# Mixing 32x64 and 32x32 matmul products within a round of a four-layer convolution stack

## The chip, the cores and the metric

The kernel runs on one NeuronCore of a Trainium2 chip. The metric is the device time of one execution in microseconds; lower is better. Before the change it is 5016.14 us, the median of 3 runs (5004.99 to 5017.03).

## The reference

The input is 4 images of 16 channels, 512 x 512, in fp32. Four layers follow one another, each `x = x + f(groupnorm(x))` with 8 groups. Layers 0 and 1 are those that the change touches:

```python
def _denoise_block(x, w1, b1, w2, b2, w3, b3, a, b, c):
    trip = _triplets(x)                # each frame with the one before and the one after it
    xf = trip.reshape(B * T, C, H, W)  # 3 input channels, 1 output channel
    o = a * _conv_reflect(xf, w1, b1, 1, 2) + b * _conv_reflect(xf, w2, b2, 2, 4) + c * _conv_reflect(xf, w3, b3, 4, 8)
    return jnp.tanh(o).reshape(B, T, H, W)
# layer 0: two such blocks, 5x5 taps at dilations 1, 2 and 4
y = _denoise_block(gn(x), ...); z = _denoise_block(y, ...)
# layer 1: activations rounded to 8-bit steps, a 3x3 convolution 16 -> 16 channels, scale and bias
x_q = jnp.round(jnp.clip(x_cl / scale_input, -n, n))
acc = lax.conv_general_dilated(x_q, w_hwio, window_strides=(1, 1), padding=((1, 1), (1, 1)), ...)
out = acc * (scale_input * scale_weight) + bias
```

Layer 2 is a 17 x 17 box filter, layer 3 a complex convolution between an FFT and its inverse.

## The kernel before

**Tiling of the array.** TensorE's 128 x 128 array is used in tiles. In layers 0 and 1 each product contracts over one strip of 32 rows (`i` = 0 to 3 in layer 0, `b` = 0 to 3 in layer 1) and writes either 64 output columns (a 32x64 product, "wide", W below) or 32 (a 32x32 product, "narrow", N below). A column half `j` (columns 0 to 63 or 64 to 127) holds one W or two N. A *round* fills the whole array once: with 8 W, or with 16 N. All moving operands are 512 fp32 columns.

**Layer 0** (`Layer0`) runs 32 groups (2 convolution blocks, 4 images, 4 groups of 4 frames), each in 6 *slots*, one for each of 6 transformed frames (`ORDER`); so 192 slots. `slot` writes down by hand, in one order for all engines, what a slot does: `products` puts the slot's products on TensorE, into one of two PSUM tiles `m`; `gather` and `activated` combine the results of the slot before on ScalarE and VectorE; `late`, `early` and `fetch` prepare later frames; `transfers` issues the slot's DMAs on SyncE, each behind one of the slot's *marks* (the last product of each round), so that they spread over the slot.

The products of a slot are listed by two constants at the top of the file. `PAIRS` has 5 pairs of neighbouring shifts that one W does together, `ALONE` 4 single shifts in 2 twos, of which each half does two N. With `e` = 0 and 1 that makes 10 rounds of W and 4 of N: 10 x 8 + 4 x 16 = 144 products. `order` runs all rounds of one shape and then all of the other, W first in slots of even `p`, N first in odd ones, so that neighbouring slots meet in the same shape. `start` is set in round 0, `stop` in the last.

**Layer 1** (`layer1`, inner function `products`) runs 64 chunks `u` of 8 image rows. A chunk has 8 rounds: for each of 4 weight blocks `d` (three taps and the residual) one round of W (`both`) and one of N (`single`). Again all four rounds of one shape come first, W first in odd chunks, N first in even ones. Loads and stores are tied to marks in the same way. `rounded` and `write` run beside it on ScalarE and VectorE.

## Time and profile before

| What | us |
|---|---|
| median of 3 runs | 5016.14 |
| the profiled execution, own time | 5011.86 |
| its span, first to last instruction | 5010.0 |
| layer 0's products (L579), first start to last end | 62.2 to 2785.9 |
| layer 1's products (L1047), first start to last end | 2825.8 to 3347.9 |
| layers 2 and 3 | about 3348 to 5010 |
| mean granted TensorE clock | 0.977 of full speed |

In the profile PE stands for the matmuls, PEld for the weight loads that go with them, DVE for VectorE, ACT for ScalarE, POOL for GpSimd and SP for SyncE; `L579` is a line of the kernel. A group's name such as `32*64 32x512 f32` gives the tile of the array (rows x columns) and the moving operand. The ends of matmuls are modelled, their starts are recorded. `l0w` are layer 0's weights, `frame` its inputs, `l1q` and `l1x` layer 1's inputs.

### The profile page before, as it was taken

Reading aid. Unit: us, or ns where it says so; the run is one execution under the profiler, and the core shown is the slowest. Engines: PE = TensorE matmul, PEld = TensorE weight load, DVE = VectorE, ACT = ScalarE, POOL = GpSimd, SP = SyncE. Lnnn points to the kernel's source line nnn. Section 1 sums busy time; section 2 is a strip of 40 time slices with the busy share of each in tenths; the row PEclk is TensorE's granted clock in tenths of the full one; section 3 lists DMA queues with packets and bytes.
Section 4 is the critical chain, followed back from the end, with each engine's and each line's share of the span. In section 5 each row is a group of like instructions: output and inputs, shape, how many; then the busy total and the mean of one; then the engine's idle time right before and its main releaser. Section 6 shows DMA issues by size and latency. Waiting matters only on the chain.

```text
span 5010.0 us, 201323 instructions
## 1 busy us (share of the span) xinstructions
PE 4727.3 (94%) x90224; PEld 2673.6 (53%) x90224; DVE 4068.3 (81%) x4639; ACT 2565.3 (51%) x4220; POOL 21.5 (0%) x90
## 2 busy tenths in 40 slices
PE   4899999999999999999999699989999989999999
PEld 1344444444444444434434345548878767777776
DVE  8888888979769999999899666655555588888887
ACT  3465656563324443444434555545444456666665
POOL 0000000000000000000000000000000000000000
PEclk9999999999999999999999899999999989999999
DMA  5656565563567777776875688876666655555553
GB/s 175 166 159 167 170 164 160 152 179 96 122 139 158 152 159 160 158 160 140 168 153 135 169 276 264 263 227 230 214 217 203 207 135 146 149 144 142 151 147 115
DMA packets 393825, 850.69 MB, mean 170 GB/s; under 512 B 70912, under 2 KB 86400, under 8 KB 384512
## 3 DMA queue, kind: packets, MB, share of 16 engines
q1 hardware_dynamic: 385456, 827.22, 61.9%
q8 instruction: 707, 11.58, 1.1%
q10 hardware_dynamic: 7504, 10.60, 0.8%
q14 instruction: 158, 1.29, 0.1%
HBM read 497.51 MB, written 340.03 MB: 167 GB/s over the span
## 4 chain that ended last, share of the span: by engine, by line
PE 76%; DVE 15%; DMA 4%; issue 2%; ACT 2%; SPq 1%; ACTq 0%; POOL 0%; DVEq 0%
PE m L579 38%; PE l1p L1047 10%; PE l2p L1154 8%; PE u L1622 5%; PE s L1563 5%; PE u L1563 4%; DVE frame L487 4%; PE u L1585 2%; PE pt L1597 2%; DVE frame L432 2%; DVE l2o L1194 2%; PE l2p L1205 1%; DVE st L1195 1%; DMA frame<-y 1%; DVE B L630 1%
## 5 line engine op out<-in xcount | busy, mean ns | idle before, releaser
L579 PE MATMUL m<-frame,l0w 32*64 32x512 f32 (+1 forms) x55296 | 2614.3, 612 | 171.6 <-DVE frame L527 62.2
L579 PEld LDWEIGHTS m<-frame,l0w 32*64 32x64 f32 (+1 forms) x55296 | 1180.2, 119 | 1604.8 <-issue 1379.8
L487 DVE SCALAR_TENSOR_TENSOR frame<-frame,frame 128x2376 f32<-128x2376 f32 x232 | 607.7, 2628 | 8.6
L1047 PE MATMUL l1p<-l1q,l_wt 32*32 32x512 f32 (+1 forms) x9216 | 432.9, 603 | 45.5 <-DVE l1q L1034 39.9
L1194 DVE TENSOR_TENSOR l2o<-l2x,l2p 128x512 f32<-128x512 f32 x256 | 172.6, 674 | 265.2 <-PE l2p L1154 265.2
L712 ACT ACTIVATE junk<-xb,neg 128x1024 f32<-128x1024 f32 x256 | 293.6, 1147 | 81.5 <-DVE top L691 31.7
L1047 PEld LDWEIGHTS l1p<-l1q,l_wt 32*32 32x32 f32 (+1 forms) x9216 | 188.5, 113 | 250.5 <-issue 210.8
L1154 PEld LDWEIGHTS l2p<-k_c_band,l2y 128*128 128x128 f32 x2048 | 256.7, 190 | 75.8 <-issue 55.1
L1183 ACT COPY l2y<-l2p 128x512 f32<-128x512 f32 x256 | 149.9, 586 | 282.0 <-PE l2p L1154 281.9
L1154 PE MATMUL l2p<-k_c_band,l2y 128*128 128x144 f32 (+1 forms) x2048 | 284.1, 292 | 6.0
L432 DVE STREAM_TRANSPOSE frame<-xp 128x1056 f32<-128x1056 f32 x128 | 261.5, 2126 | 29.9 <-ACT xp L401 29.9
L1154 PE MATMUL l2p<-k_c_band,l2n 128*128 128x144 f32 (+1 forms) x2048 | 267.8, 291 | 14.1 <-DMA l2x<-x 7.1
L1154 PEld LDWEIGHTS l2p<-k_c_band,l2n 128*128 128x128 f32 x2048 | 261.1, 196 | 15.0 <-ACT l2n L1172 11.1
L1622 PE MATMUL u<-k_c_hil,zt 128*128 128x128 f32 x2048 | 255.9, 278 | 0.0
L1622 PEld LDWEIGHTS u<-k_c_hil,zt 128*128 128x128 f32 x2048 | 238.4, 192 | 2.1 <-issue 0.8
L1598 ACT COPY zt<-pt 128x512 f32<-128x512 f32 x256 | 131.4, 599 | 208.3 <-PE pt L1597 208.3
L1528 DVE TENSOR_TENSOR xc<-l3n,k_c_tab 128x2048 f32<-128x2048 f32 x64 | 146.7, 2292 | 107.3 <-ACT l3n L1512 107.3
L1062 ACT ACTIVATE l1o<-l1p,k_l_bias,l_osc 128x1024 f32<-128x1024 f32 x128 | 147.2, 1200 | 137.9 <-PE l1p L1047 132.3
L1641 DVE SCALAR_TENSOR_TENSOR l3o<-u,l3t 128x256 f32<-128x256 f32 x512 | 192.3, 425 | 22.3 <-ACT l3t L1633 19.5
L1064 DVE BATCH_NORM_STATS2 l1st<-l1o 128x6 f32<-128x512 f32 x256 | 158.1, 680 | 54.1 <-ACT l1o L1062 54.1
L1028 ACT ACTIVATE l1t<-l1x,l1own,l1own 128x1024 f32<-128x1024 f32 x128 | 151.7, 1233 | 89.9 <-DMA l1x<-x 83.6
L1047 PE MATMUL l1p<-l1x,l_wt 32*32 32x512 f32 (+1 forms) x3064 | 195.4, 594 | 0.0
(314 smaller groups left out, 6341.6 us busy)
## 6 DMA issues: line engine op xcount, KB each, us to landing
y<-y SPq DMA_DIRECT2D x256, 264.0 KB
xb<-in_x SPq DMA_DIRECT2D x512, 128.0 KB
x<-l1o SPq DMA_DIRECT2D x256, 256.0 KB
l2x<-x SPq DMA_DIRECT2D x64, 1024.0 KB
x<-l2o SPq DMA_DIRECT2D x64, 1024.0 KB
l3x<-x SPq DMA_DIRECT2D x256, 256.0 KB
out<-l3o SPq DMA_DIRECT2D x256, 256.0 KB
l1x<-x SPq DMA_DIRECT2D x252, 256.0 KB
```

What stands on the lines that cost most here:

```text
L432: nc.vector.transpose(v[:, :, :, h, 1:17].rearrange("p k u m -> p k m u"), xp)
L487: self.nc.vector.scalar_tensor_tensor(o, x, f, y, ALU.mult, ALU.add)
L579: return nc.tensor.matmul(ps[at, i, :].rearrange("p (k c m) -> p k c m", k=nc_, c=2), w[PX * i : PX * i + PX, weights], source(i, d, e, j) ...
L712: nc.scalar.activation(junk, xs[h], f, bias=neg, accum_out=self.out_sums[b][n][:, 2 * t + h : 2 * t + h + 1])
L1028: nc.scalar.activation(t[:, at], x[:, at], AF.Identity, bias=own[1], scale=own[0])
L1047: ins = nc.tensor.matmul(ps[at : at + hi - lo, b, :], wt[rows, d, lo:hi], qs[v % 3][rows, k, d : d + W] if d < 3 else raws[v][rows, k], st ...
L1064: nc.vector.bn_stats(st[b][:, u, :], o[:, b, :])
L1154: nc.tensor.matmul(ps[:, lo:hi], lhs[:, k, at : at + P], band[:, j : j + hi - lo], start=(k == 0), stop=(k == 3), skip_group_check=True,)
L1194: nc.vector.tensor_add(o[:, hb, :], xt[:, hb, :], ps)
L1563: nc.tensor.matmul(ps[b][32 * j : 32 * j + 32], f[rows, n, j, :], x[rows, j, :], start=(i == 0), stop=(i == 2 and tag == "s"), skip_group_ ...
L1622: nc.tensor.matmul(po[:, bass.ts(k, P)], zt[:, b, k ^ 1, :], hil[:, k, :], start=False, stop=(k == 3), skip_group_check=True,)
L1641: nc.vector.scalar_tensor_tensor(o[:, v].rearrange("p k u -> p u k"), po[:, HW:W].rearrange("p (u k) -> p u k", u=2), s, t.rearrange("p (u ...
```

## The change

Each column half now has its own list of rounds. `SINGLES` says in which of a slot's 14 rounds half 0 and half 1 do their N; the two sets have no round in common. So a slot has 8 mixed rounds, in which one half does W and the other N (4 W and 8 N), and 6 rounds of W alone. Within a round the code still goes through the row strips `i` and, in each, through the halves `j`; a mixed round therefore runs W, N, N, W, N, N, ... or N, N, W, N, N, W, ... along the strips. The order no longer depends on the slot's parity. In layer 1 every round is mixed: in even rounds half 0 does N and half 1 W, in odd ones the other way round. The products, their weights, operands and results are the same in number and kind, as are the marks.

```diff
--- before.py
+++ after.py
@@ -32,6 +32,7 @@
 PAIRS = ((4, 0), (2, 1), (0, 2), (-2, 3), (1, 5))
 ALONE = (((-4, 4), (6, 0)), ((-1, 6), (3, 5)))
 NPB = 2 * len(DELTA)
+SINGLES = (0, 4, 7, 11), (2, 5, 9, 12)
 NQ = 6
 ORDER = (1, 2, 3, 4, 0, 5)
 KN = 9 * 264
@@ -561,8 +562,11 @@
         ps = self.psum.tile([P, 4, 512], F32, name=f"m{self.now}", tag="m")
         v = gr["v"][q]
         w = self.w[q]
-        runs = [(e, pair) for e in range(2) for pair in PAIRS], [(e, two) for e in range(2) for two in ALONE]
-        order = [(wide, *what) for wide in ((1, 0) if p % 2 == 0 else (0, 1)) for what in runs[1 - wide]]
+        order = []
+        for singles in SINGLES:
+            pairs = [(e, *pair) for e in range(2) for pair in PAIRS]
+            alone = [(e, two) for e in range(2) for two in ALONE]
+            order.append([alone.pop(0) if n in singles else pairs.pop(0) for n in range(14)])
 
         def source(i, d, k, j):
             if conv:
@@ -581,20 +585,21 @@
                 w[PX * i : PX * i + PX, weights],
                 source(i, d, e, j),
                 start=(n == 0),
-                stop=(n == len(order) - 1),
+                stop=(n == 13),
                 skip_group_check=True,
             )
 
-        for n, (wide, e, what) in enumerate(order):
-            base = len(DELTA) * PX * e
+        for n in range(14):
             for i in range(4):
                 for j in range(2):
-                    if wide:
+                    e, *what = order[j][n]
+                    base = len(DELTA) * PX * e
+                    if len(what) == 2:
                         d, o = what
                         at = base + PX * o
                         ins = product(slice(64 * j, 64 * j + 64), i, slice(at, at + 64), d, e, j, n)
                         continue
-                    for u, (d, o) in enumerate(what):
+                    for u, (d, o) in enumerate(what[0]):
                         at = base + PX * o
                         out = slice(64 * j + PX * u, 64 * j + PX * u + PX)
                         ins = product(out, i, slice(at, at + PX), d, e, j, n)
@@ -1036,10 +1041,10 @@
             def products(u):
                 ps = psum.tile([P, B, W], F32, name=f"l1p_{u}", tag="ps")
                 marks.clear()
-                both = ((0, 0, 0, 64), (64, 2, 0, 64))
-                single = ((0, -1, 32, 64), (32, 1, 0, 32), (64, 1, 32, 64), (96, 3, 0, 32))
-                order = [(tiles, d) for tiles in ((both, single) if u % 2 else (single, both)) for d in range(4)]
-                for n, (tiles, d) in enumerate(order):
+                wide = ((0, 0, 0, 64),), ((64, 2, 0, 64),)
+                single = ((0, -1, 32, 64), (32, 1, 0, 32)), ((64, 1, 32, 64), (96, 3, 0, 32))
+                for n in range(8):
+                    d, tiles = n // 2, (*(single, wide)[n % 2][0], *(wide, single)[n % 2][1])
                     for b in range(B):
                         for at, k, lo, hi in tiles:
                             v, k = (u - 1, 3) if k < 0 else (u, k)
```

## The prediction

> **What bounds the kernel now.** I read the busy shares first, then the chain of work that ended last, then the matmul groups with shapes kept apart.

> ```profile
> PE 4727.3 (94%) x90224; PEld 2673.6 (53%) x90224; DVE 4068.3 (81%) x4639; ACT 2565.3 (51%) x4220; POOL 21.5 (0%) x90
> PE m L579 38%; PE l1p L1047 10%; PE l2p L1154 8%; PE u L1622 5%; PE s L1563 5%; PE u L1563 4%; DVE frame L487 4%; PE u L1585 2%; PE pt L1597 2%; DVE frame L432 2%; DVE l2o L1194 2%; PE l2p L1205 1%; DVE st L1195 1%; DMA frame<-y 1%; DVE B L630 1%
> L579 PE MATMUL m<-frame,l0w 32*64 32x512 f32 x30720 | 1720.8, 598 | 70.3 <-DVE frame L527 62.2 <-DVE frame L487 4.2 <-issue 3.9
> L579 PE MATMUL m<-frame,l0w 32*32 32x512 f32 x24576 | 907.0, 629 | 101.4 <-DVE frame L487 52.8 <-issue 39.0 <-DVE C L637 8.7
> ```

> TensorE is nearly always busy, and 48% of the chain is the two lines that the change reorders (L579, L1047). The counts give the passes: 192 slots x 144 products = 27,648, yet 55,296 matmuls ran, so a product is two passes, each with its own weight load. What sits close behind TensorE in layer 0 is VectorE, 642 us of the last 685:

> ```profile
> 2100.00:2785.00 685.00, 657.03 (x13815) 295.15 (x13807) 642.45 (x615) 299.25 (x518) 0.00 (x0) 0.98 0.70 149
> ```

> The question is what a change of product shape costs, so I read layer 1's timeline, where tile names keep neighbouring rows apart (columns: start, length, then the instructions):

> ```profile
> 2999.43 1.06 PE L1047 MATMUL l1p<-l1x,l_wt 32*32 32x512 f32 x12
> 3000.42 2.83 PE L1047 MATMUL l1p<-l1q,l_wt 32*64 32x512 f32 x48
> 3003.05 1.06 PE L1047 MATMUL l1p<-l1x,l_wt 32*64 32x512 f32 x16
> 3003.91 2.78 PE L1047 MATMUL l1p<-l1q,l_wt 32*64 32x512 f32 x48
> 3006.48 1.06 PE L1047 MATMUL l1p<-l1x,l_wt 32*64 32x512 f32 x16
> 3007.48 2.98 PE L1047 MATMUL l1p<-l1q,l_wt 32*32 32x512 f32 x82
> ```

> Where the shape stays, the next row starts 0.20 us before the modelled end of the last (3003.05 against 3000.42 + 2.83); at both changes of shape only 0.06 to 0.07 before it. In the single records that distance is 0.070 us (to 0.002) at practically all of the 192 changes in layer 0 and 64 in layer 1, measured from the product that started last, wherever in the array it sat, although the starts of the last burst spread over 0 to 0.39 us. At the end of a 32x32 run the last product is in row strip 3 of column half 1; the next 32x64 one is in strip 0 of half 0, shares no cell with it, and still waits. Its weights wait too. The stretch ahead of the change at 1493.66, and one of the same length inside the new run (columns: length, then busy time and count of PE and of PEld on L579):

> ```profile
> 1493.14:1493.65 0.51, 0.51 (x18) 0.00 (x0) 1.00 0.69 225
> 1494.16:1494.67 0.51, 0.51 (x24) 0.26 (x16) 1.00 0.83 265
> ```

> No load at all for half a microsecond, against 16. I read it as one mode for the whole array: a change of shape waits until every product in flight has ended.

> **The change, part by part.** It adds and removes no product, load, transfer or wait: still 80 products of 32x64 and 64 of 32x32 in each slot, 14 marks for the transfers to hang on (8 in a layer-1 chunk), and the same VectorE, ScalarE, GpSimd and SyncE queues. What changes is how often the shape alternates in TensorE's stream. Before, 193 stretches of one shape in layer 0 and 65 in layer 1. In the built program of the changed kernel there are 12,288 in layer 0: 6,144 of two 32x32 products, 4,608 of one 32x64, 768 of eight, 384 of two and 384 of ten; and 3,585 in layer 1: 1,538 of two 32x32, 255 of four, 1,536 of one 32x64, 256 of two. A mixed round is W N N W N N ... along the four row strips (W wide, N narrow), so it has about eight changes.

> A stretch costs its first pass to its second on the same tile, then from the last start to the first start of the next shape. Both are in the records: after the change at 1493.661 the second 32x64 pass starts at 1494.141 (0.480, the weights not preloaded); after the one at 1511.471 the second 32x32 pass at 1511.926 (0.455). The second pass has its weights and lasts 0.587; less 0.070 makes 0.517, which is layer 1's start-to-start at a change. Neighbours start 0.007 apart. So one W: 0.480 + 0.517 = 0.997 us; two N: 0.455 + 0.007 + 0.517 = 0.979; two W 1.004; eight W 1.043; four N 0.993; ten W, where two tiles come twice, two more passes of 0.434, so 1.872.
> Layer 0: 6,144 x 0.979 + 4,608 x 0.997 + 768 x 1.043 + 384 x 1.004 + 384 x 1.872 = 12,515 us. Layer 1: 1,538 x 0.979 + 255 x 0.993 + 1,536 x 0.997 + 256 x 1.004 = 3,547.
> Against that, their products now take 62.2 to 2785.9 = 2,723.7 us and 2825.8 to 3347.9 = 522.1. The rest of the 5,010.0 us span is 1,764.2 and isn't touched. Sum: 1,764 + 12,515 + 3,547 = 17,826, with the 1.9 us around the span (5,011.86 profiled) 17,828: I say 17,830. The median of the runs shown is 0.1% above the profiled run, far below any bound here.

> What the change could win is inside this sum. A pure 32x32 round took 8.184 us for eight (1.02 each) against 0.88 for a 32x64 round (17.28 for 19.5), since sixteen small products with their loads come one per 17 ns twice over. That, 4 x 0.14 us a slot, is 110 us in layer 0, and is lost entirely if the array drains within each round. The other engines hide nothing of it: VectorE's 12 to 13 us a slot lie under a slot of 12,515 / 192 = 65 us. Transfers hang on marks that come later, and so does the SyncE queue behind them, but their readers are later by as much.

> [...]

> **The rivals.** (a) Free: a change waits only for the tiles it overlaps, and the halves go their own ways. Decided by whether the first W starts while the other half's N are in flight. For it: equal-shaped tiles do overlap. Against it: the 0.070 us above. Price: a slot of 14 x 0.884 = 12.4 instead of 13.27 us (17.81 + 8.72 for two slots undisturbed), at most -170 us in layer 0, of which VectorE (2,430 of its 2,724 us busy) may leave half; layer 1 about 64 x (4 x 0.14 + 0.3) = -55. So 4,790 to 4,880, say 4,830: faster.
> (b) Each half remembers its shape, so only a half's own change drains. Then a slot has about 12 single and 2 double drains. A drain between whole rounds costs 17.81 - 40 x 0.442 = 0.13 to 8.72 - 8.18 = 0.53 us, a double one 1.0 more: 12.4 + 6.6 = 19.0 us a slot, +930; layer 1, double at all eight rounds, +610. About 6,550. Nothing in the trace separates halves; it is against the loads' standing still for everything.
> (c) Full drain, and the clock stays at half. The clock was low only behind idle stretches of 2.5 us and more, and the drains leave 0.1. But a busy TensorE was seen with a low clock:

> ```profile
> 4035.00:4040.00 5.00, 5.00 (x16) 3.45 (x16) 4.20 (x6) 0.59 (x1) 0.00 (x0) 0.50 0.28 48
> ```

> and no row shows a stream with only one or two tiles of the array at work. A pass takes 1.053 there instead of 0.587: 16,062 x 1.79 + 1,764 = 30,500.

> **How the numbers follow.** Full drain at full clock 82%, (c) 4%, (b) 6%, (a) 7%, nothing measurable 1%. The likeliest case alone: at least 0.441 + 0.517 = 0.958 a stretch with the loads hidden, 17,300 us; at most 0.480 + 0.552, the longest common start-to-start, and 0.1 for what no row shows, 20,000. Stretched to 16,000 and 21,000 for passes that pair otherwise than I think and for some time at a low clock, it holds eight in ten alone; no bound of another case lies near. Faster by over 0.3% is (a): 7%; within 0.3%, about what this measurement can tell from no change: 1%; slower 92%.

> **What would show it.** Right: slots of 65 us; the idle of PEld counted under "issue" up many times over; PEld and PE with the same counts; VectorE's share near 25%, its busy time unchanged; clock near 1. One row strip's W and N starting within 0.02 us of each other would make it wrong at once: then (a). Slots near 19 us are (b), matmuls of 1.05 us (c).

## The result

The changed kernel takes 32,147.5 us (median of 4 runs, 32,146.46 to 32,151.41) against 5,016.59 before (median of 4), a ratio of 6.4099 with a 95% interval of 6.4008 to 6.419. The forecast was 17,830, in a range of 16,000 to 21,000: slower, as forecast, but 1.8 times the forecast and far outside the range.

From the page of the changed kernel: the busy shares, the clock in 40 slices (9 is nine tenths or more), and the chain of work that ended last, by engine and by line:

```profile
PE 31982.9 (99%) x90224; PEld 5169.4 (16%) x90224; DVE 4079.0 (13%) x4639; ACT 2555.7 (8%) x4220; POOL 21.3 (0%) x90
...
PEclk9999999999999999999999999999999999999999
...
PE 99%; DVE 1%; issue 0%; DMA 0%; SPq 0%; ACT 0%; ACTq 0%; DVEq 0%
PE m L583 74%; PE l1p L1052 21%; PE l2p L1159 1%; PE u L1627 1%; PE s L1568 1%; PE u L1568 1%; PE u L1590 0%; PE pt L1602 0%; DVE l2o L1199 0%; PE l2p L1210 0%; DVE st L1200 0%; PE pr L1612 0%; SPq L211 0%; DMA x<-xb 0%; DMA l0w<-frame 0%
```

The counts of instructions are those of before, and so is the work of VectorE and ScalarE. TensorE alone sets the time, with 74% of the chain in layer 0's products and 21% in layer 1's. Now the two groups of layer 0 with shapes kept apart (after the count: busy us, mean ns of one):

```profile
L583 PE MATMUL m<-frame,l0w 32*64 32x512 f32 x30720 | 12759.9, 1082 | 0.0
L583 PE MATMUL m<-frame,l0w 32*32 32x512 f32 x24576 | 11777.0, 1056 | 62.5 <-DVE frame L528 62.5
```

Before, the same matmuls had 598 and 629 ns. Nearly all now have 1,055 to 1,110, the length that some 1,300 of them had before, nearly all while the clock stood at 0.5. Yet the PEclk row shows full speed, and the mean granted clock is given as 0.999. That row can't be believed here: the trace's list of clock entries holds none before 30.5 ms, where layer 2 begins, and a time without an entry counts as full speed. The kernel before shows the same on a small scale: its list begins at 66.9 us, and the 40 matmuls that ended before that took 1,056 ns and more, though the row counts them at full speed.

The pause at a change of shape is there as foreseen, and scaled. Two stretches of the same length on L583 of the changed kernel, ahead of a change and from it on (length, busy time and count of PE and of PEld, then PEclk, DMA share and GB/s):

```profile
9001.28:9002.25 0.97, 0.97 (x16) 0.00 (x0) 1.00 0.37 135
9002.26:9003.23 0.97, 0.97 (x12) 0.18 (x4) 1.00 0.00 0
```

No weight is loaded for 0.97 us, until the last product has ended, then two narrow ones start with their loads. The stretches of one shape are just those counted from the program: 12,288 and 3,585. Two N take 1.847 us from their first start to the next shape's (6,144 times, 11,346 us), one W 1.893 (4,608 times, 8,724 us), and the next start comes 0.070 us before the modelled end of the last product, as before. Layer 0's stretches come to 23,673 us and layer 1's to 6,710, counted to the start of the last one in each; with the untouched 1,764 that is 32,148 of a span of 32,149.6. So nothing else was added, and the question left is why every pass ran at half speed.

### The profile page after: what moved, and what is told of

It is laid out like the page before. It is cut to its first block, busy times and chain, and to the rows that moved or that the text cites. A ratio compares the mean times of both kernels' runs of the same rounds, so it can differ in the third digit from the quotient of the medians.

```text
span 32149.6 us, 201322 instructions
## 1 busy us (share of the span) xinstructions
PE 31982.9 (99%) x90224; PEld 5169.4 (16%) x90224; DVE 4079.0 (13%) x4639; ACT 2555.7 (8%) x4220; POOL 21.3 (0%) x90
## 4 chain that ended last, share of the span: by engine, by line
PE 99%; DVE 1%; issue 0%; DMA 0%; SPq 0%; ACT 0%; ACTq 0%; DVEq 0%
PE m L583 74%; PE l1p L1052 21%; PE l2p L1159 1%; PE u L1627 1%; PE s L1568 1%; PE u L1568 1%; PE u L1590 0%; PE pt L1602 0%; DVE l2o L1199 0%; PE l2p L1210 0%; DVE st L1200 0%; PE pr L1612 0%; SPq L211 0%; DMA x<-xb 0%; DMA l0w<-frame 0%
## 5 line engine op out<-in xcount | busy, mean ns | idle before, releaser
L583 PE MATMUL m<-frame,l0w 32*32 32x512 f32 (+1 forms) x55296 | 23674.9, 1070 | 62.5 <-DVE frame L528 62.5
L583 PEld LDWEIGHTS m<-frame,l0w 32*32 32x32 f32 (+1 forms) x55296 | 3094.8, 171 | 20641.0 <-issue 20575.2
L1052 PE MATMUL l1p<-l1q,l_wt 32*32 32x512 f32 (+1 forms) x9216 | 5154.1, 1065 | 38.3 <-DVE l1q L1039 36.9
L1052 PE MATMUL l1p<-l1x,l_wt 32*32 32x512 f32 x3064 | 1798.6, 1065 | 0.0
L1052 PEld LDWEIGHTS l1p<-l1q,l_wt 32*32 32x32 f32 (+1 forms) x9216 | 640.6, 157 | 4442.5 <-issue 4439.3
L635 DVE TENSOR_TENSOR B<-A,m 128x1024 f32<-128x1024 f32 x64 | 77.9, 1218 | 3670.4 <-PE m L583 3670.4
L641 DVE TENSOR_TENSOR D<-C,m 128x1024 f32<-128x1024 f32 x64 | 78.0, 1218 | 3543.2 <-PE m L583 3543.2
L1035 DVE TENSOR_SCALAR l1q<-l1t 128x2048 f32<-128x2048 f32 x64 | 78.5, 1227 | 3512.4 <-PE l1p L1052 3512.3
L1052 PEld LDWEIGHTS l1p<-l1x,l_wt 32*32 32x32 f32 x3064 | 220.7, 157 | 1462.1 <-issue 1462.1
L691 DVE STREAM_TRANSPOSE zr<-z 128x1024 f32<-128x1024 f32 x128 | 151.5, 1222 | 1296.7 <-ACT z L666 1296.7
L1159 PE MATMUL l2p<-k_c_band,l2n 128*128 128x144 f32 (+1 forms) x2048 | 269.5, 292 | 14.2 <-DMA l2x<-x 7.2
```

The costliest lines, as they stand in the source:

```text
L583: return nc.tensor.matmul(ps[at, i, :].rearrange("p (k c m) -> p k c m", k=nc_, c=2), w[PX * i : PX * i + PX, weights], source(i, d, e, j) ...
L691: nc.vector.transpose(zr[:, h].rearrange("p s (k j) -> p k s j", j=16), z.rearrange("p (k r) -> p k r", r=32))
L1052: ins = nc.tensor.matmul(ps[at : at + hi - lo, b, :], wt[rows, d, lo:hi], qs[v % 3][rows, k, d : d + W] if d < 3 else raws[v][rows, k], st ...
L1159: nc.tensor.matmul(ps[:, lo:hi], lhs[:, k, at : at + P], band[:, j : j + hi - lo], start=(k == 0), stop=(k == 3), skip_group_check=True,)
```

## The experiments

All but the last two kernels leave layer 0 as before, so that layer 1 alone is asked; it lies behind 40 us in which TensorE is idle and begins with the clock at 0.5 (2790.7 to 2835.1 in the trace before). Before, its products took 522 us. Each of these kernels was run once; the last two have 4 and 10 runs. `...` marks lines left out of an edit.

**Layer 1 mixed alone.** The changed kernel's loop for layer 1 in the kernel before:

```diff
...
+for n in range(8):
+    d, tiles = n // 2, (*(single, wide)[n % 2][0], *(wide, single)[n % 2][1])
     for b in range(B):
         for at, k, lo, hi in tiles:
```

> Layer 0 as before, layer 1 mixed as in the changed kernel. In the changed kernel layer 1's 3,585 stretches of one shape took 6,711 us, all at the slow pass of 0.85 us. Theory 'asleep by its own pattern' (a layer that mixes within a round cannot keep or get the full clock): layer 1 again 6,710 us, total 5,012 - 522 + 6,710 = 11,200. Rival 'inherited' (the clock was lost in layer 0, and layer 1 only kept what it found): stretches of 0.98 to 1.00 us, layer 1 about 3,550, total 8,040.

Measured: 11,215.1 us, layer 1 6,712. The slow clock comes with layer 1's own order, whatever layer 0 did. Here the list of clock entries is complete, and it says so. A stretch of 100 us within layer 1 (columns: length, then busy time and count of PE, PEld, DVE, ACT and POOL, the clock, DMA share, GB/s):

```profile
3000.00:3100.00 100.00, 100.00 (x186) 12.37 (x184) 4.93 (x6) 4.56 (x4) 0.00 (x0) 0.50 0.05 13
```

TensorE is busy for all of it at a clock of 0.50, with only 186 matmuls.

**Half the layer pure, half mixed.**

```diff
 order = [(tiles, d) for tiles in ((both, single) if u % 2 else (single, both)) for d in range(4)]
+if u >= NYB // 2:
+    mixed = (*single[:2], both[1]), (both[0], *single[2:])
+    order = [(mixed[n % 2], n // 2) for n in range(8)]
```

> Layer 0 as before; layer 1's chunks 0 to 31 as before, chunks 32 to 63 mixed, so that the mixing begins with the clock at full. 'Wake only' (a mixed stream cannot raise the clock, but an awake array stays awake, since the drains leave it idle for only 0.1 us): 32 chunks of 55.4 us instead of 8.15, total about 6,530. 'Asleep by its own pattern': the clock falls within some 10 us of the first mixed chunk, 32 chunks of 105 us, total about 8,110.

Measured: 8,111.7 us. The clock falls, 3.4 us after the first mixed product, at 3102.8 (same columns):

```profile
3096.00:3099.00 3.00, 3.00 (x115) 1.84 (x97) 0.06 (x1) 2.38 (x2) 0.00 (x0) 1.00 0.96 285
3099.30:3102.40 3.10, 3.10 (x33) 0.51 (x8) 2.99 (x4) 2.30 (x2) 0.00 (x0) 1.00 0.79 254
3103.10:3107.00 3.90, 3.90 (x9) 0.60 (x10) 2.00 (x3) 2.37 (x2) 0.00 (x0) 0.50 0.00 1
```

The first line is the last pure chunk, the second the first mixed stretches at full clock, the third the same order at half. In the second, the two stretches that lie wholly in the full clock, one of each kind, took 0.979 us (two N) and 0.997 (one W), to the nanosecond what the forecast had. The next takes 1.144, as the clock falls in it, and from 3103.1 on they take 1.85 and 1.89, for good.

**The same rounds, half by half.** All N of one half, then all W of the other (`single` and `wide` as in the change):

```diff
...
-for b in range(B):
-    for at, k, lo, hi in tiles:
+halves = ((single[0], wide[1]), (single[1], wide[0]))[n % 2]
+for b, tiles in [(b, tiles) for tiles in halves for b in range(B)]:
+    for at, k, lo, hi in tiles:
```

> Layer 0 as before; layer 1 mixed, but in each round all N of the one column half (8 products) run before all W of the other (4 products): 16 stretches a chunk instead of 56, each filling half of the array, with the same pause at each change. Full drain at each change holds in any case. 'Fill' (the clock goes by how much of the array is at work): somewhere between; at full clock a stretch is about 1.02 us, layer 1 about 1,045 and the total 5,540. 'Pauses' (it goes by the share of time in which products stream, 0.85 of 1.0 us as in the mixed rounds): half clock, 1.92 us a stretch, layer 1 1,965, total 6,460.

Measured: 5,540.45 us, layer 1 1,048, at full clock. Each stretch has the pause of the mixed ones and is as long (1.018 us); it only has all four row strips of a half at work instead of one:

```profile
3000.00:3100.00 100.00, 100.00 (x1184) 18.94 (x1190) 42.30 (x103) 29.64 (x27) 0.00 (x0) 1.00 0.41 130
```

Pauses are out as the cause of the slow clock. That N and W stand in different halves, with no cell in common, spares no pause: of 1,023 changes here, 1,020 have 0.516 to 0.520 us from the last start to the next, and the first three, still at half clock, 0.985 to 0.987.

**Whole rounds in turn.** N and W rounds alternate, eight changes a chunk:

```diff
-order = [(tiles, d) for tiles in ((both, single) if u % 2 else (single, both)) for d in range(4)]
+order = [(tiles, d) for d in range(4) for tiles in (single, both)]
```

> Layer 0 as before; layer 1 with rounds of one shape throughout, but N and W rounds in turn: 8 changes of shape a chunk instead of 1, each stretch a whole round that fills the array, of the same length in time (two passes and a drain) as a mixed stretch. 'Fill': full clock, 4 x (1.04 + about 1.2) = 9 us a chunk, layer 1 575, total about 5,070. 'Pauses': half clock as in the mixed rounds, 15.8 us a chunk, layer 1 1,010, total 5,500.

Measured: 5,059.02 us, layer 1 563, at full clock. An N round with its change takes 1.093 us, a W round 1.078, so that seven further changes a chunk cost 0.6 us. A change between rounds that fill the array is cheap, 0.09 us each here. An estimate from layer 1 of the trace before comes near: 0.517 us from the last start to the first of the next shape, less the 0.434 from one W pass to the next on its tile, is 0.083.

**No pauses, less of the array.** One change of shape a chunk as before, but row strip after row strip, then tile after tile (in these two and the next two kernels the marks are set at eight even distances in a chunk's products):

```diff
-for n, (tiles, d) in enumerate(order):
-    for b in range(B):
+# l1_strip
+order = [(4 * s + d, b, d, shapes[s]) for s in range(2) for b in range(B) for d in range(4)]
+# l1_tile
+order = [(4 * s + d, b, d, (t,)) for s in range(2) for b in range(B) for t in shapes[s] for d in range(4)]
+for n, b, d, tiles in order:
```

> Layer 0 as before; layer 1 with the shapes in the order of before (one change a chunk), but one row strip after the other, so that a quarter of the array is at work and nothing pauses. If TensorE doesn't look past a strip: 64 passes of 0.442 us a chunk at full clock, layer 1 1,810 us, total 6,300; at half clock 3,630 and 8,120. 'Fill' with a threshold under a quarter, or 'pauses and fill together': full clock. 'Fill' with a threshold above a quarter: half clock.

> The same, but tile after tile: the products of one tile follow one another, an eighth (W) or a sixteenth (N) of the array at work, as in a mixed stretch, but without pauses and with one change of shape a chunk. If TensorE doesn't look past a tile: 192 passes of 0.442 us a chunk, layer 1 5,430 us, total 9,920 at full clock; 10,900 and 15,400 at half. 'Fill alone': half clock. 'Pauses and fill together': full clock.

Measured: 6,535.24 and 10,004.82 us; layer 1 2,032 and 5,511, both at half clock throughout. The strip order:

```profile
3000.00:3100.00 100.00, 100.00 (x628) 30.05 (x624) 16.51 (x21) 16.63 (x15) 0.00 (x0) 0.50 0.26 83
```

TensorE is never idle, changes shape once in some 32 us, and still gets half the clock. No pauses are needed for that. Both times fell between the two that were expected, because later products did start ahead of earlier ones (look-ahead): tile after tile, two matmuls ran at a time, 0.007 us apart; strip after strip, 64 W passes in 15.7 us and 128 N passes in 16.0 make 3.5 W tiles of 8 and 6.8 N tiles of 16 at work, 43% of the array both times. Within a strip only 2 W or 4 N tiles have products, so those of the next strip start while earlier ones still wait. It showed among products of one shape only: all 64 changes of the strip order have 0.985 to 0.987 us from the last start to the next, the full pause at half clock.

**Column after column.** The same, with all four row strips next to one another in the order:

```diff
-order = [(4 * s + d, b, d, shapes[s]) for s in range(2) for b in range(B) for d in range(4)]
+order = [(4 * s + d, b, d, (t,)) for s in range(2) for t in shapes[s] for d in range(4) for b in range(B)]
```

> Layer 0 as before; layer 1 without pauses as in the strip order, but one column tile after the other, all four row strips in each. The strip order had 43% of the array's tiles at work (64 W and 128 N passes of 0.853 us in 31.75 us a chunk), yet stayed at half clock, while by-halves with 45% at that clock woke. 'Share of tiles': the same 43%, half clock, layer 1 about 2,030 us, total 6,530. 'Share of row strips' (all four at work here and in by-halves, one to two of four in the strip order): full clock, layer 1 about 1,030, total 5,530.

Measured: 5,321.23 us, layer 1 828, at full clock:

```profile
3000.00:3100.00 100.00, 100.00 (x1492) 42.44 (x1488) 42.41 (x52) 34.84 (x31) 0.00 (x0) 1.00 0.51 165
```

Faster than either figure, since look-ahead filled more of the array for W than expected (64 passes of 0.427 us in 4.6 us, 74% of the tiles). But the clock rose at 2831.1, 4 us after the first product, with N alone and little more than a quarter of the tiles at work. All entries in the list of clocks lie on a grid of 3.41 us (in the kernel before the low ones last 3.41, 6.83, 10.24 us and so on); the table has, from the single records, the last steps before the clock rose, and steps of orders in which it didn't; each matmul counts as 0.853 us, the distance between two on the same tile at half clock:

| order, step of 3.41 us at half clock | share of the tiles at work | share of the time with any pass | matmuls started | then |
|---|---|---|---|---|
| columns, 2827.7 | 0.28 | 1.0 | 20 | rose |
| by halves, 2834.7 | 0.44 | 0.91 | 24 | rose |
| by halves, 2831.3 | 0.28 | 0.65 | 18 | stayed low |
| strips, W, steady | 0.49 | 1.0 | 14 to 16 | stayed low |
| strips, N, steady | 0.48 | 1.0 | 28 to 32 | stayed low |
| tiles, N, steady | 0.12 | 1.0 | 7 or 8 | stayed low |
| mixed, steady | 0.11 to 0.18 | 0.91 to 0.95 | 4 to 10 | stayed low |

Neither the share of the tiles (0.28 rose, 0.49 didn't), nor the time (1.0 didn't, 0.91 did), nor the number of matmuls (20 rose, 32 didn't) tells them apart. The number of row strips that stream at once does, if they stream nearly all of the time: by the order of the products four in the first two lines, about two of four in the strip order (3.9 of 8 W tiles, two to a strip), one in the last two. The kernel before agrees: its N rounds use all four strips, and a step in which they streamed for 0.82 of the time (804.1, 0.72 of the tiles) stayed low, while one with 0.91 (2579.1, 0.82 of the tiles) rose. So does layer 0 of the changed kernel: its six rounds of W alone in a slot do fill the array, but between 5,000 and 6,000 us no window of 3.41 us has it filled for more than 0.48 of its time.

**Strips after pure chunks.**

```diff
 order = [(4 * s + d, b, d, shapes[s]) for s in range(2) for b in range(B) for d in range(4)]
+if u < NYB // 2:
+    order = [(4 * s + d, b, d, shapes[s]) for s in range(2) for d in range(4) for b in range(B)]
```

> Layer 0 as before; layer 1's chunks 0 to 31 in the order of before, 32 to 63 strip after strip, so that the strips begin with the clock at full. If the clock goes by the same bar up and down, it falls: 32 chunks of 31.75 us instead of 8.15, total about 5,770. If an awake array needs less to stay awake: 32 chunks of 16.5, total 5,285.

Measured: 5,762.7 us, as for one bar, but not in the way expected. The first strip chunk begins with N at 3091.8 and keeps the full clock for 9.3 us, through two whole steps of the grid with 0.41 and 0.42 of the tiles at work. At 3101.1 the shape changes to W, after a drain; that step has 0.27 (columns as above):

```profile
3090.00:3100.00 10.00, 10.00 (x199) 5.73 (x185) 6.06 (x7) 6.22 (x6) 0.00 (x0) 1.00 0.64 217
3100.00:3110.00 10.00, 10.00 (x56) 3.28 (x52) 1.23 (x1) 0.00 (x0) 0.00 (x0) 0.67 0.29 80
```

At 3103.4 the clock drops, and the N runs after it, at 0.48 of the tiles, never raise it. So the bar to stay awake is lower than the one to wake: an awake array kept its clock at 0.42 in the strip order and lost it at 0.27 there and at 0.16 when mixed. That the clock merely falls late is unlikely, as the mixed half lost it after a single step.

**The change with its halves grouped, in both layers.** The changed kernel with one loop order turned round in each layer:

```diff
-for i in range(4):
-    for j in range(2):
+for j in range(2):
+    for i in range(4):
         e, *what = order[j][n]
...
+    d, halves = n // 2, ((single, wide)[n % 2][0], (wide, single)[n % 2][1])
-for b in range(B):
+for tiles, b in [(tiles, b) for tiles in halves for b in range(B)]:
```

> The changed kernel with one thing altered in both layers: inside a round all strips of half 0 run before all strips of half 1, instead of alternating along the strips. 16 stretches a slot instead of 64 (8 of eight N, 6 of eight W, 2 of sixteen W); in layer 1 neighbouring stretches of one shape merge into whole rounds. By the stretches measured so far (eight N 1.018 us, a W round 1.077, a second 0.88 more) a slot takes 8 x 1.018 + 6 x 1.077 + 2 x 1.96 = 18.5 us, layer 0 3,555 to 3,650, layer 1 562, at full clock: total 5,880 to 5,980. If instead mixing as such, by halves, costs the clock: layer 0 6,800 and more, total above 9,000.

Measured: 5,892.35 us, a ratio to before of 1.1741 (1.1722 to 1.1761). Layer 0's stretches take 3,558 us, layer 1 570. Layer 0 with shapes apart:

```profile
L583 PE MATMUL m<-frame,l0w 32*64 32x512 f32 x30720 | 2079.5, 617 | 0.0
L583 PE MATMUL m<-frame,l0w 32*32 32x512 f32 x24576 | 1694.9, 607 | 63.1 <-DVE frame L528 63.1
```

The same rounds, products and halves as in the changed kernel, with 16 changes a slot instead of 64 and the clock back: 26,255 of the 27,131 us that the change cost are gone. What remains is 18.5 us a slot for an average of 14.2 before (13.3 undisturbed). The records put it together from eight stretches of N at 1.03 us on average, in which by the order half the array stands still, six rounds of W at 1.07 and two double ones at 1.93.

**The aim of mixing, another way.** An N round takes 1.02 us against 0.88 for W. Here the strips run innermost in every round, with the order of shapes as before:

```diff
-for i in range(4):
-    for j in range(2):
+for j in range(2):
+    for u, (d, o) in enumerate((what,) if wide else what):
+        for i in range(4):
...
-for b in range(B):
-    for at, k, lo, hi in tiles:
+for at, k, lo, hi in tiles:
+    for b in range(B):
```

> Both layers with the shapes in the order of before; inside each round the row strips run innermost, so that neighbouring products lie in different strips. Asks whether the 1.02 us of an N round against 0.88 of a W round, which mixing was to spread out, comes from the loads of neighbouring products sharing a strip. If so, N rounds near 0.88: layer 0 up to 110 us less, of which VectorE may take half, layer 1 up to 35 less: 4,870 to 4,950. If the pace is that of issuing one product after the other: within 0.3% of before.

Measured: 5,015.4 us, ratio 0.9996 (0.9984 to 1.0008). The undisturbed N run of two slots is as long as before (10th percentile 8.737 against 8.721 us). The pace doesn't come from neighbours in a strip; what sets it stays open (one product per 17 ns twice over, the prediction's account, would be 0.54 us for sixteen, not 1.02). No version tried beats the kernel before.

## Why the prediction was wrong

- *One mode for the whole array; a change of shape waits until every product in flight has ended.* Right. All 15,871 changes show it (0.984 to 0.986 us from the last start to the next), and by halves it holds for products with no cell in common. Rivals (a) and (b) are out: with (b), within a mixed round nothing would drain.
- *The count of stretches.* Right: 12,288 and 3,585, of the kinds named.
- *The price of a stretch, 0.979 and 0.997 us.* Right at full clock, as the half-mixed layer showed in its first 3 us. In the changed kernel 1.847 and 1.893: the pass 0.85 instead of 0.43, the drain 0.986 instead of 0.517. This is the term of the sum that was mis-sized, by 1.89, on 16,062 us.
- *The clock was low only behind idle stretches of 2.5 us and more, and the drains leave 0.1; so full clock 82%, (c) 4%.* This is the step that failed. The observation was nearly true of the trace before (the shortest idle stretch ahead of a low clock was 1.9 us, not 2.5), but in all of that kernel's long streams the array was filled, so it couldn't tell an idle TensorE from a thinly used one. The prediction says itself that no row shows one or two tiles at work; so nothing in the trace spoke for 82 against 4, and the overlooked term is the clock's dependence on how the array is filled. What the runs showed in its place: with mostly one row strip at work the clock never rose (layer 1 mixed, 6,712 us at 0.50), and fell from 1.00 to 0.50 where it was full (half pure, half mixed, at 3102.8). The row quoted for (c), 5.00 us busy at a clock of 0.50, was no case of it: eight matmuls of two columns came ahead of full ones there, and the clock was back at 1.00 in the 5 us that follow. Rival (c) is what happened. Its 30,500 was 5% low, as it scaled a stretch by the length of a matmul (1.79); start to start they grew by 1.89.
- *The other engines hide nothing, transfers come later and cost nothing; the rest of the span isn't touched.* Right: the stretches and the 1,764 us add up to the span within 2 us.
- *What would show it.* Slots came out at 23,673 / 192 = 123 us, not 65, and matmuls at 1.056 to 1.110 us, near the 1.05 said for (c); VectorE's share is 13%, not 25%, with its busy time unchanged; "clock near 1" held on the page and was false.

Busy time alone doesn't tell the clock either: the strip order, with TensorE busy 100.00 of 100.00 us in the stretch shown, ran at 0.50 for 2,032 us.

What stays open is what exactly sets the clock. Row strips streaming at once fit every order that was run, with a bar to wake between about two of four all the time and four for nine tenths of it; but how far TensorE looks ahead, and so how many strips stream, is inferred from counts, and no order with three strips was run. The bar to stay awake lies somewhere between 0.27 and 0.42 of the tiles in the strip order.

## What to carry to other kernels

Products of 32x64 and of 32x32 didn't run side by side on TensorE in any kernel here, not even in separate halves (1,023 changes, each with the pause), so such shapes belong in runs that fill the array, where a change cost 0.1 to 0.5 us. A stream that kept about one row strip of the array at work paid twice, for the empty tiles and with a clock of 0.50, although TensorE was never idle (tile after tile, 5,511 us for 522). When matmuls of a known form have a new length (here 1,056 and 1,082 ns for 629 and 598, under a clock given as 0.999), believe it before the clock row.
